# A long convolution's Toeplitz pipeline: an order left to a scheduler, and one written out in slots of four channels

## The chip, the core and the metric

The kernel runs on one core of one Trainium2 chip. TensorE multiplies matrices, VectorE (DVE in the profile) and ScalarE (ACT) work elementwise, GpSimd (POOL) and SyncE (SP) here mostly issue transfers. The metric is the device time of one launch in microseconds.

## The reference

The program is a model of two layers, each with two mixers and a feed-forward part, over x of 2 sequences, 2048 tokens and 256 channels, in f32. The change lies in one mixer of the second layer, and only that matters here:

- x is normalized and projected to 512 inner channels and 512 gates: `xz = norm(x) @ W_in.T`.
- The inner channels go through a causal convolution of four taps with a bias, then Silu: xs.
- Each channel is convolved, causally along its sequence, with a kernel of its own, 1024 taps long (`k_ssm`): y.
- `(y + D_skip * xs) * silu(gate)` is projected back by `W_out` and added to x.

## The kernel before

The method is `sublayer_c`. The 4096 tokens are cut into eight chunks of 512 (`NCH`, `CH`), the 512 inner channels into four blocks of 128 (`E`, index e).

The long convolution is a matmul for each channel. With the sequence in tiles of 128 tokens, tile i of y is the sum over nine shifts m of a 128 x 128 Toeplitz matrix and tile i - m of x. The channel's x, 16 tiles of two sequences, is the stationary operand of 32 columns; a piece of 128 columns of the channel's Toeplitz rows streams past it. Four channels share the array, each with 32 output partitions, so a group of four channels is 4 x 9 matmuls (`convolve`, L1160). Each f32 matmul has two records in the trace. A block has 32 groups, the stage 128. Four groups fill a PSUM tile and leave together (`leave`, L1171: one copy by ScalarE and one transfer to DRAM, c_yd); four groups are called a quartet below.

The Toeplitz rows of a group are made by `kernels` (L1102) in a tile toep of 128 partitions x 4 channels. Two transfers bring 32 partitions each, one for two of the channels on SyncE's queue, one for the other two on ScalarE's. In each half the other 96 partitions are shifted copies: two by VectorE (L1111, L1112), two by ScalarE (L1113, L1114), the second of each pair reading what the first wrote. The pool c_kb has three such tiles, so the loads for a group can start only when the convolution three groups before is done.

Beside that, one chunk's work for the block after (`produce`, `turn`) and the block before (`finish`, `project`) is put into each quartet. `produce` (L1128) projects a chunk (TensorE, L1133), copies it to SBUF (ScalarE, c_xi, L1139), runs the four taps (VectorE, c_acc, L1142 and L1144) and Silu (ScalarE, c_xs, L1146), and writes c_xs to DRAM; `turn` (L1150) transposes it and VectorE puts it into the ring c_x (L1156). `finish` (L1178) reads y and xs back through GpSimd's queue, makes the gate (TensorE, L1186; ScalarE's Silu, L1188), and joins them on VectorE (L1189, L1190); `project` (L1193) multiplies by W_out into ps_o and adds to x (L1201). c_xi, c_acc, c_xs, c_yc and ps have two or three buffers, ps_o one.

Block 0 has no finished block beside it, block 3 none to produce; block 0 is produced ahead of the loop, block 3 is finished behind it.

In what order an engine works is settled by `manual_schedule`. Before, it names TensorE only: TensorE follows the order of the program's text, and a scheduler arranges the others by its own estimates, also across the bounds of stages. Each engine's own stream is then fixed: an instruction that waits holds up all behind it.

Of the kernel before, what the change touches and what calls it, by code (L numbers as in the profile page):

```python
# [17 lines left out]
AF = mybir.ActivationFunctionType  # L18
ALU = mybir.AluOpType
AX = mybir.AxisListType  # L20
PSUM = bass.MemoryType.PSUM
DRAM = bass.MemoryType.DRAM

P = 128
# [4 lines left out]
CH = 512  # L29
NCH = NT // CH  # L30
# [29 lines left out]
def new(pool, shape, name, **kw):  # L60
    return pool.tile(list(shape), F32, name=name, tag=name, **kw)


class Kernel:
# [1007 lines left out]
    def sublayer_c(self):  # L1072
# [7 lines left out]
        tc, nc = self.tc, self.nc  # L1080
        V, A, G = nc.vector, nc.scalar, nc.gpsimd
        E, TAPS = 4, L_CONV // P
        Q = P // 4
        W = L_CONV + P + P - Q
        with ExitStack() as c:
            dp = c.enter_context(tc.tile_pool(name="c_dram", bufs=1, space=DRAM))
            yd = dp.tile([E * P, NB, B, P], F32, name="c_yd", tag="c_yd")
            xd = dp.tile([E * P, NT], F32, name="c_xd", tag="c_xd")
            kp = c.enter_context(tc.tile_pool(name="c_k", bufs=1))
            xT = new(kp, [P, 2, NT], "c_xT")  # L1090
            wi = self.load(kp, "C_W_inT", pat="(k p) n -> p k n", p=P)
            wo = self.load(kp, "C_W_outT", pat="(k p) n -> p k n", p=P)
            cw = self.load(kp, "C_conv_w", pat="(k p) n -> p k n", p=P)
            cb = self.load_cols(kp, "C_conv_b")
            dk = self.load_cols(kp, "C_D_skip")
            xring = [new(kp, [P, P, TAPS + NB, B], f"c_x{j}") for j in range(2)]
            for t in xring:
                G.memset(t[:, :, 0:TAPS], 0.0)
            kb = c.enter_context(tc.tile_pool(name="c_kb", bufs=3))
            kr = self.a["C_krev"]  # L1100

            def kernels(e, g):  # L1102
                t = new(kb, [P, 4, W], "toep")
                for r in range(2):
                    first = kr.offset + (e * P + 4 * g + 2 * r) * KREV
                    (nc.scalar if r else nc.sync).dma_start(
                        out=t[r * (P - Q) : r * (P - Q) + Q, 2 * r : 2 * r + 2],
                        in_=bass.AP(kr.tensor, first, [[1, Q], [KREV, 2], [1, W]]),
                    )
                a, b = t[:, 0:2], t[:, 2:4]  # L1110
                V.tensor_copy(a[Q : 2 * Q, :, 0 : W - Q], a[0:Q, :, Q:W])  # L1111
                V.tensor_copy(a[2 * Q : P, :, 0 : W - 3 * Q], a[0 : 2 * Q, :, 2 * Q : W - Q])  # L1112
                A.copy(b[2 * Q : 3 * Q, :, Q:W], b[3 * Q : P, :, 0 : W - Q])  # L1113
                A.copy(b[0 : 2 * Q, :, 3 * Q : W], b[2 * Q : P, :, Q : W - 2 * Q])  # L1114
                return t

            with tc.tile_pool(name="c_ln", bufs=2) as lp, tc.tile_pool(name="c_pl", bufs=2, space=PSUM) as pl:
                self.norm_transpose(lp, pl, lambda i: self.x[:, i, :], list(range(NI)), xT)
            tp = c.enter_context(tc.tile_pool(name="c_t", bufs=2))
            xp = c.enter_context(tc.tile_pool(name="c_xin", bufs=3))  # L1120
            pp = c.enter_context(tc.tile_pool(name="c_ps", bufs=2, space=PSUM))
            pt = c.enter_context(tc.tile_pool(name="c_pt", bufs=1, space=PSUM))
            pc = c.enter_context(tc.tile_pool(name="c_pc", bufs=2, space=PSUM))
            po = c.enter_context(tc.tile_pool(name="c_po", bufs=1, space=PSUM))
            c.enter_context(tc.manual_schedule(engines={mybir.EngineType.PE}))
            last = [None]

            def produce(e, ch):  # L1128

                b, i0, cs = ch // 4, ch % 4 * 4, slice(ch * CH, (ch + 1) * CH)  # L1130
                ps = new(pp, [P, CH], "ps")
                for k in range(2):
                    nc.tensor.matmul(ps, wi[:, k, e * P : (e + 1) * P], xT[:, k, cs], start=k == 0, stop=k == 1)  # L1133
                xin = new(xp, [P, 3 + CH], "c_xi")
                if i0 == 0:
                    V.memset(xin[:, 0:3], 0.0)
                else:
                    V.tensor_copy(xin[:, 0:3], last[0][:, CH : CH + 3])
                A.copy(xin[:, 3:], ps)  # L1139
                last[0] = xin  # L1140
                acc = new(tp, [P, CH], "c_acc")
                V.tensor_scalar(acc, xin[:, 0:CH], cw[:, e, 0:1], cb[:, e : e + 1], ALU.mult, ALU.add)  # L1142
                for j in range(1, 4):
                    V.scalar_tensor_tensor(acc, xin[:, j : j + CH], cw[:, e, j : j + 1], acc, ALU.mult, ALU.add)  # L1144
                xs = new(tp, [P, CH], "c_xs")
                A.activation(xs, acc, AF.Silu)  # L1146
                G.dma_start(out=xd[e * P : (e + 1) * P, cs], in_=xs)
                return e, ch, xs

            def turn(e, ch, xs):  # L1150

                b, i0 = ch // 4, ch % 4 * 4
                ps = new(pt, [P, 4, P], "ps_t")
                for j in range(4):
                    nc.tensor.transpose(ps[:, j, :], xs[:, j * P : (j + 1) * P], self.ident)
                V.tensor_copy(  # L1156
                    xring[e % 2][:, :, TAPS + i0 : TAPS + i0 + 4, b], ps.rearrange("p j c -> p c j")
                )

            def convolve(e, g, t, ps):  # L1160
                x = xring[e % 2]
                for m in range(TAPS + 1):
                    for j in range(4):
                        lo = L_CONV - m * P + j // 2 * (P - Q)
                        nc.tensor.matmul(  # L1165
                            ps[j * 32 : (j + 1) * 32, g % 4, :],
                            x[:, 4 * g + j, TAPS - m : TAPS - m + NB, :].rearrange("p i b -> p (i b)"),
                            t[:, j, lo : lo + P], start=m == 0, stop=m == TAPS,
                        )

            def leave(e, g, ps):  # L1171

                ys = new(tp, [P, 4, P], "c_ys")
                A.copy(ys, ps[:, :, ::-1])
                rows = slice(e * P + 4 * g, e * P + 4 * g + 16)
                A.dma_start(out=yd[rows].rearrange("(s j) i b t -> (j i b) s t", j=4), in_=ys)

            def finish(e, ch):  # L1178
                b, i0, cs = ch // 4, ch % 4 * 4, slice(ch * CH, (ch + 1) * CH)
                yc, xs = new(tp, [P, CH], "c_yc"), new(tp, [P, CH], "c_xs")  # L1180
                G.dma_start(out=yc.rearrange("p (i t) -> p i t", t=P), in_=yd[e * P : (e + 1) * P, i0 : i0 + 4, b])
                G.dma_start(out=xs, in_=xd[e * P : (e + 1) * P, cs])
                ps = new(pp, [P, CH], "ps")
                z0 = E * P + e * P
                for k in range(2):
                    nc.tensor.matmul(ps, wi[:, k, z0 : z0 + P], xT[:, k, cs], start=k == 0, stop=k == 1)  # L1186
                sz = new(tp, [P, CH], "c_acc")
                A.activation(sz, ps, AF.Silu)  # L1188
                V.scalar_tensor_tensor(yc, xs, dk[:, e : e + 1], yc, ALU.mult, ALU.add)  # L1189
                V.tensor_tensor(yc, yc, sz, ALU.mult)  # L1190
                return e, ch, yc

            def project(e, ch, yc):  # L1193
                for j0 in range(0, 4, 2):
                    ps = new(po, [P, 2, D], "ps_o")
                    for j in (j0, j0 + 1):
                        nc.tensor.matmul(
                            ps[:, j - j0], yc[:, j * P : (j + 1) * P], wo[:, e, :], start=True, stop=True
                        )
                    i = ch * 4 + j0  # L1200
                    V.tensor_tensor(self.x[:, i : i + 2, :], self.x[:, i : i + 2, :], ps, ALU.add)  # L1201

            due = []

            def later(step, *todo):

                for f, args in due:
                    f(*args)
                due[:] = [(step, a) for a in todo]

            for ch in range(NCH):
                t = produce(0, ch)
                later(turn, t)
            later(turn)
            for e in range(E):
                for g in range(P // 4):
                    t = kernels(e, g)
                    if g % 4 == 0:
                        ps = new(pc, [P, 4, P], "ps_c")
                    convolve(e, g, t, ps)  # L1220
                    if g % 4 == 3:
                        leave(e, g - 3, ps)
                    if g % 4 == 0:
                        work = []
                        if e + 1 < E:
                            work.append((turn, produce(e + 1, g // 4)))
                        if e > 0:
                            work.append((project, finish(e - 1, g // 4)))
                    elif g % 4 == 2:
                        for f, args in work:  # L1230
                            f(*args)
            for ch in range(NCH):
                t = finish(E - 1, ch)
                later(project, t)
            later(project)


    def ternary_weights(self, pool):
# [459 lines left out]
```

## Time and profile before

| | us |
|---|---|
| median of 3 runs | 13912.62 (13908.2 to 13919.0) |
| profiled execution | 13913.98, its span 13912.3 |
| norm ahead of the stage | 10969.9 to 11012.5 |
| eight chunks of block 0 | 11012.5 to 11051.8 |
| 128 groups | 11051.8 to 11938.3 |
| end of block 3 | 11938.3 to 11986.0 |

In the profile, PE is TensorE's matmuls and PEld its weight loads; a q behind an engine's name is its queue of transfers, whose issue does not count as busy. A line of instructions gives start, length, engine, line, operation, output and inputs, and in brackets the idle time ahead of it and what ended that. A line of waits gives the engine and what waited, what it waited for, the sum in us, how often, and the longest. PEclk is the granted clock of TensorE as a part of the full one.

### The profile page before, as it was taken

To read this page: it belongs to the slowest core of one execution; us is meant where nothing else is said; L and a number is where in the kernel's file an instruction comes from. 1 tells how busy PE (TensorE), PEld (TensorE's weight loads), DVE (VectorE), ACT (ScalarE), POOL (GpSimd) and SP (SyncE) were. 2 spreads that over 40 slices of the span, in tenths; PEclk is the share of its full clock that TensorE was granted. 3 is DMA by queue.
4 is the path that set the end of the run, shared out by engine and by line. 5 is a ranking of instruction groups with operands and counts; after the bars stand their busy time and mean duration, and the time that the engine had idled before them with its cause. 6 is when DMAs were issued, how large, how long until landed. Compare 5 with 4: busy or idle time off the path is not lost. (4 is left out here: it accounts for less than half of the span.)

```text
span 13912.3 us, 263001 instructions
## 1 busy us (share of the span) xinstructions
PE 5521.0 (40%) x66344; PEld 3798.1 (27%) x66344; DVE 10663.1 (77%) x65491; ACT 9306.1 (67%) x45234; POOL 432.4 (3%) x496
## 2 busy tenths in 40 slices
PE   4222222222222222222222222222289766778888
PEld 2111111111111111111111111111255444544445
DVE  6888888888888888888888888888857655555555
ACT  3777777777777777777777777777626366434444
POOL 0000000000000000000000000000000000131110
PEclk7555555555555555555555555555579778889999
DMA  3000000000000000000000000000000144242210
GB/s 80 14 15 16 17 14 17 14 17 17 14 17 14 17 17 14 17 14 17 17 14 17 14 17 17 14 17 14 14 13 1 41 123 132 62 94 35 33 32 19
DMA packets 334776, 382.28 MB, mean 27 GB/s; under 512 B 207074, under 2 KB 247081, under 8 KB 332212
## 3 DMA queue, kind: packets, MB, share of 16 engines
q1 hardware_dynamic: 289204, 281.11, 8.8%
q10 hardware_dynamic: 29184, 49.82, 1.3%
q0 software_dynamic: 14848, 34.36, 0.9%
q8 instruction: 533, 8.73, 0.3%
q14 instruction: 1007, 8.25, 0.2%
HBM read 307.96 MB, written 52.46 MB: 26 GB/s over the span
## 5 line engine op out<-in xcount | busy, mean ns | idle before, releaser
L410 PE MATMUL hc<-hs,mean 128*32 128x2 f32 x16384 | 588.2, 203 | 7116.8 <-DVE hs L480 7052.2
L410 PEld LDWEIGHTS hc<-hs,mean 128*32 128x32 f32 x16384 | 412.7, 140 | 7328.8 <-DVE hs L480 7263.8
L475 DVE TENSOR_TENSOR p<-p,ir 128x64 f32<-128x64 f32 x4096 | 739.0, 222 | 1065.4 <-ACT ir L463 1065.4
L459 ACT ACTIVATE lm<-m 128x64 f32<-128x64 f32 x2048 | 466.2, 228 | 1216.3 <-DVE m L451 1216.3
L493 PE MATMUL yps<-cs,hist 128*64 128x8 f32 x8192 | 1225.0, 259 | 13.0 <-DVE hs L480 13.0
L391 ACT ACTIVATE bx<-dx,tc 128x64 f32<-128x64 f32 x4098 | 1169.4, 332 | 0.1
L1522 ACT ACTIVATE d_p<-ps_e 128x512 f32<-128x512 f32 (+3 forms) x1280 | 599.4, 537 | 756.1 <-PE ps_o L1503 534.2
L493 PEld LDWEIGHTS yps<-cs,hist 128*64 128x64 f32 x8192 | 1033.2, 218 | 45.1 <-DVE hs L480 13.4
L418 ACT ACTIVATE sq<-hc 128x2 f32<-128x2 f32 x2048 | 353.2, 172 | 794.0 <-PE hc L410 794.0
L480 DVE CUSTOM_DVE_ANT_0 hist<-p,sg 128x64 f32<-128x64 f32 x4096 | 764.5, 224 | 22.5 <-ACT rm L470 4.2
L442 DVE TENSOR_TENSOR p<-p,fac 128x64 f32<-128x64 f32 x4096 | 741.6, 222 | 8.9 <-DVE p L437 6.6
L477 DVE SCALAR_TENSOR_TENSOR p<-e,p 128x64 f32<-128x64 f32 x4096 | 740.6, 222 | 9.9 <-ACT sg L469 7.8
L444 DVE TENSOR_TENSOR p<-p,bx 128x64 f32<-128x64 f32 x4096 | 727.5, 219 | 2.5
L439 ACT ACTIVATE fac<-ngd,ci 128x64 f32<-128x64 f32 x2048 | 711.8, 348 | 1.0 <-DVE p L436 1.0
L436 DVE SCALAR_TENSOR_TENSOR p<-hist,ea 128x64 f32<-128x64 f32 x2048 | 461.1, 225 | 321.8 <-ACT ea L429 321.8
L429 ACT ACTIVATE ea<-ex 128x64 f32<-128x64 f32 x2048 | 524.3, 256 | 102.7 <-DVE ex L424 7.0
L1515 PE MATMUL ps_e<-d_qt,d_kt 128*128 128x512 f32 (+3 forms) x1280 | 558.1, 445 | 44.3 <-ACT d_p L1522 35.5
L472 ACT ACTIVATE ld<-e 128x64 f32<-128x64 f32 x2048 | 548.2, 268 | 0.0
L410 PE MATMUL hd<-hs,mean 128*32 128x2 f32 x16384 | 544.3, 193 | 0.0
L473 ACT ACTIVATE k<-rm 128x64 f32<-128x64 f32 x2048 | 544.1, 266 | 0.0
L1472 PE MATMUL ps_m<-d_kt,d_qt 128*128 128x512 f32 (+3 forms) x1280 | 499.9, 438 | 99.1 <-DVE d_part L1477 39.9
L1165 PE MATMUL ps_c<-toep,c_x 128*32 128x128 f32 x9216 | 407.5, 341 | 306.6 <-ACT toep L1114 304.9
(452 smaller groups left out, 22795.9 us busy)
## 6 DMA issues: line engine op xcount, KB each, us to landing
ng<-dtd SPq DMA_DIRECT2D x258, 256.0 KB, 3.7
dx<-dxd SPq DMA_DIRECT2D x258, 256.0 KB, 4.2
toep<-in_C_krev ACTq DMA_DIRECT2D x128, 312.0 KB, 4.7
toep<-in_C_krev SPq DMA_DIRECT2D x128, 312.0 KB, 4.7
d_kt<-d_kd SPq DMA_DIRECT2D x128, 128.0 KB, 4.1
d_qt<-d_qd SPq DMA_DIRECT2D x128, 128.0 KB, 3.8
y<-ys SPq DMA_DIRECT2D x512, 8.0 KB, 1.9
c_xd<-c_xs POOLq DMA_DIRECT2D x32, 256.0 KB, 4.5
```

The lines of the kernel that those rows point to most:

```text
L391: A.activation(bx[o][:, k2], tg[j][2][:, k], AF.Identity, scale=tg[j][0][:, k2, k : k + 1], bias=0.0 if k2 else SMALL,)
L410: nc.tensor.matmul(out[r : r + 32], mean[:, r : r + 32], hs[i], start=True, stop=True)
L439: A.activation(fac, ngd, AF.Exp, scale=ci)
L442: V.tensor_tensor(p[:, k2], p[:, k2], fac, ALU.mult)
L444: V.tensor_tensor(p[:, k2], p[:, k2], bx[o][:, k2], ALU.add)
L472: A.activation(ld, e, AF.Ln, scale=-1.0, bias=1.0)
L475: V.tensor_tensor(p[:, k2], p[:, k2], ir, ALU.mult)
L477: V.scalar_tensor_tensor(p[:, k2], e, -1.0, p[:, k2], ALU.add, ALU.mult)
L480: V.tensor_tensor_reduce(out=hn[:, k2], in0=p[:, k2], in1=sg, scale=-1.0, scalar=0.0 if k2 else J * SMALL, op0=ALU.mult, op1=ALU.add, accu ...
L493: nc.tensor.matmul(yps[:, k, :], hist[g][:, k, k2], tg[g][3][:, k2, k], start=k2 == 0, stop=k2 == 1)
L1515: nc.tensor.matmul(s[:, q0:], ks[kt // 4][:, hh, kt % 4 * P : (kt % 4 + 1) * P], q[:, hh, q0:], start=True, stop=not diag,)
L1522: A.activation(pr[:, q0:], s[:, q0:], AF.Exp, scale=0.25)
```

## The change

`manual_schedule()` now holds for all engines. The closures are cut into smaller steps, and the loop over 128 slots writes out in what order every engine meets them. In slot s:

- SyncE issues both loads for slot s+2 (`load_toep`); ScalarE issues none.
- TensorE first gets a piece of the chunk work: in slot 0 of a quartet the projection of the next block's chunk (`x_project`), in slot 1 the gate of the block before (`y_gate`), in slot 3 the transposes (`x_turn`) and the output projection (`y_project`); then it convolves slot s.
- VectorE and ScalarE fill the Toeplitz tile for slot s+1 (`fill_toep`), then take their share of the chunk: in slot 0 the copy out of the quartet before (`leave`), the loads of y (`y_load`), the copy c_xi and two taps (`x_first`); in slot 1 the gate's Silu (`y_silu`) and two taps (`x_rest`); in slot 2 the Silu of c_xs (`x_silu`) and the join (`y_join`); in slot 3 the ring (`x_keep`) and the add (`y_add`).

The write of c_yd goes through GpSimd's queue instead of ScalarE's. ps_o has two buffers instead of one. The first Toeplitz tile is filled behind the eight chunks of block 0. c_kb keeps its three tiles.

```diff
-                    (nc.scalar if r else nc.sync).dma_start(
+                    nc.sync.dma_start(
...
+            def fill_toep(s):
+                t = toeps[s]
                 a, b = t[:, 0:2], t[:, 2:4]
                 V.tensor_copy(a[Q : 2 * Q, :, 0 : W - Q], a[0:Q, :, Q:W])
+                A.copy(b[2 * Q : 3 * Q, :, Q:W], b[3 * Q : P, :, 0 : W - Q])
                 V.tensor_copy(a[2 * Q : P, :, 0 : W - 3 * Q], a[0 : 2 * Q, :, 2 * Q : W - Q])
-                A.copy(b[2 * Q : 3 * Q, :, Q:W], b[3 * Q : P, :, 0 : W - Q])
                 A.copy(b[0 : 2 * Q, :, 3 * Q : W], b[2 * Q : P, :, Q : W - 2 * Q])
...
-            po = c.enter_context(tc.tile_pool(name="c_po", bufs=1, space=PSUM))
-            c.enter_context(tc.manual_schedule(engines={mybir.EngineType.PE}))
+            po = c.enter_context(tc.tile_pool(name="c_po", bufs=2, space=PSUM))
+            c.enter_context(tc.manual_schedule())
...
-                A.dma_start(out=yd[rows].rearrange("(s j) i b t -> (j i b) s t", j=4), in_=ys)
+                G.dma_start(
+                    out=yd[4 * s : 4 * s + 16].rearrange("(s j) i b t -> (j i b) s t", j=4), in_=ys
+                )
...
+            load_toep(0)
+            load_toep(1)
+            x_project(0, 0)
             for ch in range(NCH):
...
+                x_first(0, ch)
+                if ch + 1 < NCH:
+                    x_project(0, ch + 1)
+                if ch:
+                    x_turn()
+                    x_keep(0, ch - 1)
+                x_rest(0)
+                x_silu(0, ch)
+            fill_toep(0)
+            x_turn()
+            x_keep(0, NCH - 1)
+            out = None
+            for s in range(32 * E):
+                e, q, r = s // 32, s % 32 // 4, s % 4
+                more, done = e + 1 < E, e > 0
+                if s + 2 < 32 * E:
+                    load_toep(s + 2)
+                if r == 0:
+                    before, out = out, new(pc, [P, 4, P], "ps_c")
+                    if more:
+                        x_project(e + 1, q)
+                elif r == 1 and done:
+                    y_gate(e - 1, q)
+                elif r == 3:
+                    if more:
+                        x_turn()
+                    if done:
+                        y_project(e - 1)
+                if s + 1 < 32 * E:
+                    fill_toep(s + 1)
+                convolve(s, out)
+                if r == 0:
+                    if before is not None:
+                        leave(s - 4, before)
+                    if done:
+                        y_load(e - 1, q)
+                    if more:
+                        x_first(e + 1, q)
+                elif r == 1:
+                    if done:
+                        y_silu()
+                    if more:
+                        x_rest(e + 1)
+                elif r == 2:
+                    if more:
+                        x_silu(e + 1, q)
+                    if done:
+                        y_join(e - 1)
+                else:
+                    if more:
+                        x_keep(e + 1, q)
+                    if done:
+                        y_add(q)
+            leave(32 * E - 4, out)
+            y_load(E - 1, 0)
+            y_gate(E - 1, 0)
             for ch in range(NCH):
...
+                y_silu()
+                y_join(E - 1)
+                if ch + 1 < NCH:
+                    y_gate(E - 1, ch + 1)
+                y_project(E - 1)
+                if ch + 1 < NCH:
+                    y_load(E - 1, ch + 1)
+                y_add(ch)
```

## The prediction

> **What bounds the kernel now.** I first found where the edited code runs: the time of the long convolution, cut into norm, first chunks, 128 groups and end (busy time by stretch).
>
> ```profile
> core 0: us, PE busy (x) PEld busy (x) DVE busy (x) ACT busy (x) POOL busy (x), PEclk, DMA share, GB/s
> 10969.90:11012.50 42.60, 17.45 (x64) 10.89 (x64) 36.55 (x127) 22.88 (x26) 3.44 (x2) 0.50 0.33 83
> 11012.50:11051.80 39.30, 24.97 (x66) 11.69 (x66) 26.52 (x48) 10.90 (x17) 4.51 (x8) 0.80 0.13 53
> 11051.80:11938.30 886.50, 558.79 (x9696) 424.43 (x9696) 497.80 (x489) 595.83 (x353) 62.78 (x74) 0.78 0.45 123
> 11938.30:11986.00 47.70, 33.99 (x104) 18.42 (x96) 21.77 (x33) 5.36 (x9) 9.24 (x14) 0.93 0.26 83
> ```
>
> The third row is 886.5 us for 128 groups, 6.93 us each. Nobody is full: ScalarE is busy 595.8 (67%), TensorE 559 at a granted clock of 0.78, VectorE 498, the transfers 45%. So it is a loop of waits. Then the waits of that stretch, TensorE's first, then ScalarE's.
>
> ```profile
> PE ps_c L1165 <- ACT toep L1114: 304.9, 79, 6.9
> ...
> ACT c_xi L1139 <- PE ps L1133: 75.1, 20, 7.7
> ACT c_xs L1146 <- DVE c_acc L1144: 59.6, 23, 4.3
> ACT toep L1113 <- DMA toep<-in_C_krev: 53.8, 38, 5.0
> ACT c_ys L1174 <- PE ps_c L1165: 40.2, 32, 5.8
> ACT c_acc L1188 <- PE ps L1186: 28.7, 8, 4.2
> ```
>
> TensorE waits 305 us for ScalarE's copies; ScalarE idles 291 us, most of it (75 + 60 + 40 + 29) for somebody who waits for it. The reason is its order, seen in the timeline of one quartet (four groups) of it:
>
> ```profile
> 11410.37 0.36 ACTq L1106 DMA_DIRECT2D toep<-in_C_krev  x1
> 11410.92 0.39 ACTq L1176 DMA_DIRECT2D c_yd<-c_ys  x1
> 11414.22 0.59 ACT L1139 COPY c_xi<-ps 128x512 f32<-128x512 f32 x1 [3.33 <-PE ps L1133]
> 11414.83 2.21 ACT L1113 COPY toep<-toep 32x2432 f32<-32x2432 f32 x1
> 11417.07 0.60 ACT L1188 ACTIVATE c_acc<-ps 128x512 f32<-128x512 f32 x1
> 11417.69 2.11 ACT L1114 COPY toep<-toep 64x2304 f32<-64x2304 f32 x1
> 11419.83 2.21 ACT L1113 COPY toep<-toep 32x2432 f32<-32x2432 f32 x1
> 11425.25 0.63 ACT L1146 ACTIVATE c_xs<-c_acc 128x512 f32<-128x512 f32 x1 [3.21 <-DVE c_acc L1144]
> ```
>
> The copy c_xi stands ahead of the next Toeplitz copy and waits for a matmul; the second copy of a pair (L1114) stands behind the Silu of c_xs, which waits for four VectorE taps. Meanwhile TensorE has nothing. Each quartet pays this; the next c_ys transfer comes at 11439.2, so a quartet is 28.3 us.
>
> **The change, part by part.** Sums are made on the profiled run: 13914.0 us for a span of 13912.3; it lies 1.4 above the median of the runs shown, 13912.6.
>
> *Same work, new order.* No matmul, copy or activation is added or dropped. I count ScalarE: a Toeplitz pair is 2.21 + 2.11 + two handovers of 0.02 = 4.36 us. A quartet adds c_ys 0.59, c_xi 0.59, Silu c_xs 0.63, and Silu of the gate 0.60 where a previous block is finished. Block 0 (no gate): 17.44 + 1.85 = 19.3. Blocks 1 and 2: 19.9. Block 3 (no x work): 18.65. With 8, 16 and 8 quartets: 154 + 318 + 149 = 622 us. That is the floor. VectorE is under it: pair 1.42 + 1.35 + 0.03 = 2.80, and per quartet 0.16 + 0.55 + 3 x 0.75 + 0.69 + 0.75 + 0.69 + 2 x 0.69 = 6.5, so 4.4 per slot against 4.98. TensorE: convolution 2.17 at full clock, and per quartet 1.88 (x) + 1.88 (gate) + 0.66 (turn) + 2.06 (output) = 6.5; 15.2 per quartet, 19 if a quarter slower.
>
> In the new order a slot's ScalarE work is: pair for the next slot, then one small piece whose input was made a slot earlier or at the head of this one. The 75, 60, 40 and 29 us should go. What is late next is the Toeplitz load.
>
> *The loads.* There are still three buffers, so the load for slot s+3 leaves when convolution s has ended; "two ahead" moves no release. What it has is: SyncE 0.1 + two issues of 0.31 (now both on SyncE; ScalarE gets rid of 128 issues and of the waits that stood ahead of its copies), then landing. The trace has medians of 4.5 (SyncE) and 4.7 (ScalarE), and up to 7.7 beside other transfers. A block 1 quartet moves 4 x 624 + 4 x 256 KB; in 22 us that is 160 GB/s against 138 now, so I take 5.0: 5.7 from release to landed.
>
> Step one quartet of blocks 1 and 2, time 0 where ScalarE begins slot 3 (its Silu of c_xs has just ended). TensorE turns and projects, 2.72 x 1.25 = 3.4, convolves 2.7 to 6.1. The buffer's next load lands at 11.8. ScalarE wants it after slot 3 (4.36) and slot 0 (5.54), at 9.9: about 2 us of stall. The load behind slot 0 (ends 11.2, lands 16.9) then meets a ScalarE that is there at 16.8; the others are in time. So about 22.0 per quartet. Block 0 and 3 lack one heavy TensorE piece; the same steps leave 0.2 and 0.45. Sum: 622 + 16 x 2.1 + 8 x 0.65 = 661, and 4 for the three block changes, where the first readback of y waits for the last write: **665 us, 221 less.**
>
> *TensorE's clock, the factor 1.25.* The trace: convolutions take 2.17 at full clock and up to 4.06 cold; after an idle of 2.5 us one came at 2.17 (at 11083), others at 3.70 and 4.06 after 2.55 and 2.80. The Trainium skill (TensorE: Matmul & The Clock Gate, Part 1) says that the clock falls to half after an idle window of some 3.4 us and is full after as long a busy one. New gaps are under 2.7, so by the rule factor 1: the same steps give 635. By the rows, between 1 and 1.5 (716). I take 1.25; both ends stay in the range.
>
> *Output write moved from ScalarE's to GpSimd's queue.* ScalarE loses 32 issues of 0.39; GpSimd gets them, ahead of the two y loads of the same slot. The trace: c_xs loads take 538 ns to issue at the end of the stage, but a median of 1447 in the middle, where one starts beside VectorE's Toeplitz copies. The skill (SBUF — State Buffer, "SBUF: two separate sides") speaks against this move: a DMA of GpSimd's queue can't write its descriptors while VectorE runs such an f32 copy, 620 ns growing to 3100. By the row each of three issues may take 0.9 more: y landed about 13 us after slot 0 began, when VectorE gets to the join (10.5 + 2.8). That costs nothing, barely. By the page's figure (estimate, +2.5 each) it is some 4 to 5 us late in each of 24 quartets, about 100 us. I take the row.
>
> *Ahead of the loop.* Three Toeplitz pairs now sit inside the norm (six ScalarE copies, 12.9 us, six VectorE, 8.4), some of it on its chain (the reciprocal at 10988.4 is 2.2 late, the group at 11003.4 waits 3): without them 6 us less. In return the first pair (4.36) comes after the last Silu, and the chunk chain is tap, Silu 0.63, copy 0.59, then 3.4 of VectorE: about 4.8 x 8 + 7 against 39.3. +6. Together 0; between -8 and +8.
>
> *The end.* 47.7 us now, with a period of 5.1 us per chunk since y loads come one behind another; two output buffers (po) and loads a chunk ahead leave join 1.44 + project 1.3 + add 1.38 = 4.1, plus a slower first write: -5.
>
> Sum: 13914.0 - 221 - 5 + 0 = 13688, on the median 13687.
>
> **The rivals.**
> *ScalarE alone is the limit.* If the clock stays full and loads land in 4.5, little but the floor stays: about 626, so 13648. For: the rule on the clock. Against: the 7.7 us landings.
> *Late y.* The join in slot 2 waits for loads held up in GpSimd's queue; TensorE's project stands ahead of its convolution. 665 + 100: 13790. For: 1447 against 538. Against: only one issue in three was slowed.
> *Cold TensorE.* Factor 1.85 everywhere: 7.0 per slot in blocks 1 and 2, 824 in all, 13847. Against: TensorE would then be busy nearly without a gap, and the trace shows full clock after such stretches.
> *Slower: the load loop.* Both loads on one queue, with the release tied to the third convolution before: at factor 1.25 the stage passes today's 886 by over 0.2% of the kernel once landing takes 12 us, since every microsecond more adds some 40 to the 128 slots. That would be 919 and over, 13941 or more. For: the engines wait for toep transfers now (120 us VectorE, 54 ScalarE). Against: no landing over 7.7 in the stretch that I looked at, transfers at half load.
> That the loads aren't earlier at all is true already, and in the sum.
>
> **How the numbers follow.** The forecast 0.60, ScalarE alone 0.14, late y 0.13, cold 0.07, slower 0.06. A measurement tells about 0.2%, 28 us, from no change. Faster: all but the last, 0.93; 0.02 for ends that just cancel; slower 0.05. The range runs from ScalarE alone, 13645, to past late y, 13800.
>
> **What would show it.** Right: the convolution stretch 640 to 700 us; ScalarE busy near 90% in it with the same 596 to 615 us; waits of ScalarE for c_acc and ps gone, what is left named toep load, once per quartet in blocks 1 and 2; TensorE clock above 0.85. Wrong: VectorE waiting for c_yc or c_xs in every quartet (late y); convolutions of 4 us (cold); toep landings over 7 us. An end over 13,885 would say that the order of ScalarE was not the cause.

## The result, and the profile after

The changed kernel takes 13715.1 us (median of 4 runs, 13709.0 to 13722.1) against 13911.9 before: a ratio of 0.9857, with a 95% interval of 0.9845 to 0.9870. That is 197 us less; 226 were forecast, and the range held it. The profiled run is 13713.6 us, its span 13711.9.

The same four stretches after (busy time by stretch; norm, first chunks, 128 groups, end):

```profile
core 0: us, PE busy (x) PEld busy (x) DVE busy (x) ACT busy (x) POOL busy (x), PEclk, DMA share, GB/s
10961.30:10994.20 32.90, 17.42 (x64) 10.58 (x64) 28.19 (x121) 9.94 (x20) 3.45 (x2) 0.50 0.43 107
10994.20:11039.80 45.60, 28.20 (x68) 12.44 (x68) 31.61 (x51) 14.62 (x20) 4.65 (x8) 0.76 0.11 47
11039.80:11738.70 698.90, 503.94 (x9694) 381.80 (x9694) 509.98 (x493) 603.46 (x357) 89.31 (x103) 0.86 0.59 155
11738.70:11783.70 45.00, 32.76 (x96) 19.32 (x96) 21.90 (x33) 5.36 (x9) 11.04 (x17) 0.90 0.30 100
```

The third row has nearly all of it: 886.5 us became 698.9. ScalarE has the same work (603 us) in less time, 86% busy instead of 67%. The norm takes 9.7 us less, the first chunks 6.3 more, the end 2.7 less: together -6. So the stage accounts for 194 us of the two profiled runs' 200; the rest lies ahead of the stage and behind it.

ScalarE's waits in the groups, after:

```profile
ACT toep L1118 <- DMA toep<-in_C_krev: 39.7, 20, 3.6
ACT toep L1118 <- DVE c_acc L1144: 18.4, 9, 2.4
ACT toep L1118 <- issue: 16.1, 6, 4.1
ACT c_ys L1194 <- PE ps_c L1185: 6.7, 3, 2.5
ACT toep L1118 <- DVE toep L1117: 3.4, 2, 2.9
```

The waits for taps and projections are nearly gone. What is left stands ahead of L1118, the first copy of a pair, which needs only its load and its buffer; the names behind the arrow change, the waiting instruction doesn't. It is some 80 us of load: in blocks 1 and 2, where ScalarE stalls, L1118 begins 0.1 us after the load that it needs has landed (median). TensorE's longest waits, after:

```profile
PE ps_t L1171 <- ACT c_xs L1164: 96.3, 24, 7.0
PE ps_c L1185 <- ACT toep L1120: 43.8, 32, 2.7
```

The 305 us for ScalarE's Toeplitz copies have become 44. The first row was 3.2 us before: now the transposes at the head of slot 3 wait for the Silu of c_xs, which stands on ScalarE behind a Toeplitz pair, and the convolution of slot 3 waits behind the transposes.

Measured from one c_ys copy to the next, a quartet takes 19.4 us in block 0, 23.7 and 24.0 in blocks 1 and 2, 19.7 in block 3; 19.5, 22.0 and 19.1 were forecast.

A stretch of block 1 (timeline, all engines) shows where the blocks in the middle lose it:

```profile
11294.08 0.76 POOL L1195 DMA_DIRECT2D c_yd<-c_ys  x1 [8.35 <-ACT c_ys L1194]
11294.84 0.76 POOL L1203 DMA_DIRECT2D c_yc<-c_yd  x1
11295.59 0.55 POOL L1204 DMA_DIRECT2D c_xs<-c_xd  x1
...
11302.98 1.42 DVE L1117 COPY toep<-toep 32x2432 f32<-32x2432 f32 x1 [2.64 <-DMA toep<-in_C_krev]
...
11305.06 2.21 ACT L1118 COPY toep<-toep 32x2432 f32<-32x2432 f32 x1 [3.65 <-DMA toep<-in_C_krev]
```

In slot 0 three transfers of GpSimd's queue start within 1.5 us; right then a convolution ends and lets the two Toeplitz loads go. They left at 11295.7 and 11296.1. VectorE, which needs the first, begins 7.3 us after that left, when it has landed; the second landed 8.9 us after it left, and ScalarE, which needs it, begins 9.0 after that, having stood for 3.65. Over blocks 1 and 2 the view of the tile gives (min, median, max)

```profile
DMA to landing us min/median/max: 3.6/6.0/8.9
```

but it knows the landing of only 48 of the 128 loads there, all of them of two of a quartet's four slots. Counted from the completion records of all 128 loads in the trace, the landing is 3.3 at the least, 5.0 in the median and 8.9 at most, where the forecast took 5.0 throughout. It depends on the slot. The second load of a pair, the one that ScalarE needs, has these medians: behind the convolution of slot 0 7.5 us, of slot 1 6.0, of slot 2 4.9, of slot 3 4.4.

ScalarE stalls before two of the four tiles of a quartet in blocks 1 and 2: 2.0 us on the mean before the tile loaded behind slot 3's convolution, which itself comes late, and 1.7 before the tile loaded behind slot 0's, whose load is slow. Before the other two it stands 0.1 or less. The forecast's steps had the first (about 2 us) and gave the second nothing (0.1).

### The profile page after: what moved, and what is told of

Read it like the earlier page. It is cut to its first block, busy times and chain, and to the rows that moved or that the text cites. A ratio compares the mean times of both kernels' runs of the same rounds, so it can differ in the third digit from the quotient of the medians.

```text
span 13711.9 us, 263042 instructions
## 1 busy us (share of the span) xinstructions
PE 5477.8 (40%) x66344; PEld 3762.0 (27%) x66344; DVE 10653.5 (78%) x65491; ACT 9294.0 (68%) x45234; POOL 460.9 (3%) x528
## 5 line engine op out<-in xcount | busy, mean ns | idle before, releaser
L432 PE MATMUL hd<-ident,ci 128*1 128x1 f32 x4096 | 386.7, 163 | 357.2 <-DVE ex L424 303.4
```

## Experiments

Two theories stood after the result. *The load loop*: with three buffers a load leaves when the convolution three slots before has ended, and the way from there to the next copy is just too long. *Late y*: the join of slot 2 waits for c_xs (32 us in 10 joins), and the output projection, TensorE's next convolution and the release of a buffer wait behind it. Of the two waits of TensorE that bear on it, the one for the join is small (17.4 us ahead of ps_o); the one for the Silu of c_xs (96.3 us) belongs to the loop. Times of the 128 groups run from the first convolution to the end of the last and are from one trace each; the whole kernel's are medians, except for the fourth buffer and the five runs that take the change apart, which ran once. Landings are counted from the completion records of all loads of a stretch.

**TensorE convolves first.**

```diff
-                if r == 0: x_project ... elif r == 1: y_gate ... elif r == 3: x_turn, y_project
                 if s + 1 < 32 * E:
                     fill_toep(s + 1)
                 convolve(s, out)
+                if r == 0: x_project ... elif r == 1: y_gate ... elif r == 3: x_turn, y_project
```

> TensorE convolves first in every slot and takes the chunk pieces (projection, gate, transposes, output projection) behind it; nothing else moves. Theory 1, the load loop: in blocks 1 and 2 the buffer of a slot comes free late because up to 3.4 us of chunk pieces stand ahead of the convolution; ScalarE's 81 us of waits ahead of the first Toeplitz copy fall below 40, quartets of blocks 1 and 2 go from 23.7 us to 20.5 to 21.5, the 128 groups from 699 to about 655. Theory 2, late y: the join still waits for its c_xs load and VectorE's next Toeplitz copy behind it, so the groups gain 10 us at most.

Measured: the groups 637.8 us, quartets of blocks 1 and 2 19.9; the kernel 13660.8 us (ratio to before 0.9811, interval 0.9795 to 0.9827). ScalarE's waits:

```profile
ACT c_xi L1152 <- PE ps L1137: 7.5, 12, 1.8
ACT c_acc L1216 <- PE ps L1210: 6.7, 4, 3.9
ACT toep L1118 <- DMA toep<-in_C_krev: 5.6, 6, 2.9
```

VectorE's join still waits, 37.5 us for c_xs instead of 32.3, and it costs next to nothing. Both stalls of ScalarE are gone (0.02 us each on the mean). So the loop is right, late y as a cause by itself is not: once the convolution doesn't stand behind the small pieces, the late join is not on the path. The edit does one thing more: the y transfers, which left within the last 1.5 us of slot 0's convolution, now leave 2.2 to 3.7 us after its end (medians), behind the Toeplitz loads. The load that ScalarE needs lands in 4.5 us there instead of 7.5; that behind slot 1 is slow in its place (6.5), but has room: ScalarE comes for it 1.5 us after it has landed.

**Loads of y a slot earlier.**

```diff
-                    if done:
+                    if done and q == 0:
                         y_load(e - 1, q)
...
                         y_add(q)
+                        if q + 1 < NCH:
+                            y_load(e - 1, q + 1)
```

> The loads of y and xs for a chunk are issued one slot earlier (end of slot 3 of the quartet before, except for the first chunk of a block). Theory 2, late y: VectorE's 32 us of waits for c_xs and most of TensorE's 34 us for VectorE's copies go, quartets of blocks 1 and 2 fall by 1.5 us or more, the groups by 25 to 35 us. Theory 1, the load loop: the join was not on the path; 10 us at most.

Measured: the groups 654.3, the kernel 13683.0 (0.9824, 0.9808 to 0.9841): 45 us from the groups, more than late y alone was to give. The wait for c_xs fell to 9.2 us. But the Toeplitz loads gained too: the y loads now leave some 8 to 9 us before the convolution of slot 0 ends, and the second load behind it lands in a median of 4.9 us in blocks 1 and 2 instead of 7.5. The stall before that tile is gone (0.04 us on the mean instead of 1.7), the one behind slot 3 stays (1.8). This run doesn't tell late y from the slow loads; the one before and the fourth buffer below do.

**The write of c_yd back on ScalarE's queue.**

```diff
-                G.dma_start(out=yd[4 * s : 4 * s + 16]...
+                A.dma_start(out=yd[4 * s : 4 * s + 16]...
```

> The write of c_yd is back on ScalarE's queue, everything else as changed. If GpSimd's queue is what makes y late (c_xs now lands in a median of 7.1 us, 5.5 before), c_xs lands about 1 to 1.5 us sooner, VectorE's waits for it halve, and the groups gain 10 to 25 us. If the queue is not the cause, the landing stays near 7 and ScalarE pays 32 issues of 0.39: same or up to 12 us more.

Measured: the groups 666.4, the kernel 13692.9 (0.9834, 0.9817 to 0.9850). c_xs lands in 3.8 us instead of 7.1, the Toeplitz loads of blocks 1 and 2 in 4.4 instead of 5.0. On GpSimd's queue the write had stood in front of the y loads and waited for c_ys; without it they leave some 9 us before slot 0's convolution ends, not beside its end. As with y early, the stall behind slot 0 goes (0.05 us) and the one behind slot 3 stays (1.5). ScalarE does pay for its issues, since none can leave before the copy c_ys has ended:

```profile
ACT c_xi L1152 <- ACT c_ys L1194: 8.4, 19, 0.5
```

This part of the change was a loss of some 32 us all the same, by one trace of each; by whole runs the intervals of the two ratios overlap a little.

**A fourth buffer.** The room for it comes from leaving out half the norm.

```diff
-            xT = new(kp, [P, 2, NT], "c_xT")
+            xT = new(kp, [P, 2, NT // 2], "c_xT")
-            kb = c.enter_context(tc.tile_pool(name="c_kb", bufs=3))
+            kb = c.enter_context(tc.tile_pool(name="c_kb", bufs=4))
...
-   xT[:, k, ch * CH : (ch + 1) * CH]
+   xT[:, k, ch % 4 * CH : (ch % 4 + 1) * CH]
```

> A fourth Toeplitz buffer. To make room for it the norm and its transposes are done for the first sequence only and both sequences are projected from it (so half the norm, some 16 us, is left out), and c_xi has two buffers. Only the 128 groups are to be read. Theory 1, the load loop: a load then leaves a slot earlier, ScalarE's 81 us of waits for toep nearly vanish, quartets of blocks 1 and 2 are near ScalarE's floor, 20 to 21 us, the groups 635 to 650. Theory 2, late y: 10 to 20 us of gain at most, the join's waits stay.

Measured: the groups 633.0, blocks 1 and 2 19.8 and 20.0 per quartet. ScalarE waits 2.1 us in all for loads, while the join waits for c_xs longer than ever:

```profile
ACT toep L1118 <- DMA toep<-in_C_krev: 2.1, 5, 0.5
DVE c_yc L1220 <- DMA c_xs<-c_xd: 48.0, 14, 8.7
```

The loads are no quicker than as changed (5.4 us in the median of blocks 1 and 2, 5.0 as changed), they only leave earlier. This is the cleanest proof of the loop: in the groups the text, the queues and the order are as changed, a load leaves a slot earlier, and c_xi has one buffer less, which can only hold work up. (The whole kernel's 13639.5 us is short of half a norm and is not compared.)

**Both: convolve first, y early.**

> TensorE convolves first in every slot, and y's loads are issued a slot earlier: both edits together. If late y and the late release of the buffer are one chain (y late, so the output projection late, so the convolution behind it late, so the load late), breaking it twice gives little over breaking it once: the groups 625 to 638 us against 638 with the first edit alone. If they are two separate losses they add up: about 593, which is under ScalarE's floor of 622 and so is not expected.

Measured: the groups 630.5, the kernel 13661.8 (0.9814, 0.9798 to 0.9831), no difference to convolving first alone that these runs can tell. Not additive: one chain, and under it ScalarE's work, 606.5 us busy of 630.5.

**Is ScalarE then the floor?** Beside both edits, VectorE makes the copies c_xi and c_ys.

```diff
-                A.copy(ys, ps[:, :, ::-1])
+                V.tensor_copy(ys, ps[:, :, ::-1])
-                A.copy(xin[:, 3:], held["x"])
+                V.tensor_copy(xin[:, 3:], held["x"])
```

> As the kernel with both edits, and the copies c_xi and c_ys are made by VectorE instead of ScalarE (24 x 0.59 and 32 x 0.58 us). If ScalarE's work is the floor of the groups now (606 us busy of 638), its 33 us come off nearly whole: the groups 600 to 610 us, ScalarE near 573 busy, VectorE near 547. If the load loop or VectorE bounds, nothing is gained: 630 or more.

Measured: the groups 615.4, a gain of 15 of the 33 us forecast (the 618 of the next text counts on to the c_ys copy behind the last convolution); ScalarE 579 us busy (573 forecast), VectorE 541. Block 0 went from 139 to 129 us (seven quartets), blocks 1 and 2 stayed (160 and 157 for eight), block 3 rose from 144 to 150. ScalarE was the floor of block 0; in the middle another limit was right below it, VectorE or, with 18.0 us of ScalarE's waits, the loads.

> TensorE convolves first, y's loads go a slot earlier, c_xi is copied by VectorE, c_ys by VectorE in block 0 only and by ScalarE elsewhere. With both copies on VectorE blocks 1 and 2 stayed at 157 to 160 us per eight quartets, where VectorE had 2.8 x 4 + 7.8 = 19.0 us of work in a quartet. If VectorE bounds them there, handing c_ys back to ScalarE brings 155, block 3 goes from 150 to 144, block 0 stays at 129: the groups about 610 us, against 618. If something else holds blocks 1 and 2 (loads, y), they stay at 158 and the groups near 615.

```diff
+                (V.tensor_copy if s < 32 else A.copy)(ys, ps[:, :, ::-1])
```

Measured: the groups 612.5 (610 forecast), blocks 1 and 2 155.7 and 156.6, block 3 147.7 (144 forecast). That is 3 us under the kernel with both copies on VectorE, too little in one trace each to say that VectorE was the limit there. The kernel takes 13635.9 us (5 runs, 13629.4 to 13641.4), 0.9800 of before (0.9786 to 0.9813), the fastest of all; its interval overlaps with those of the versions with TensorE convolving first, with both edits and with both copies on VectorE.

```profile
11045.90:11658.40 612.50, 480.53 (x9689) 358.81 (x9689) 526.85 (x524) 589.58 (x326) 106.52 (x103) 0.94 0.66 177
```

ScalarE is busy 96% of the groups here. With this much work on ScalarE, no order can give more than the other 23 us.

**What made the gain?** Five runs took the change apart.

The text of before with the order of all engines fixed, `manual_schedule()` and nothing else:

> The kernel before, with the order of its text fixed for all engines (the one word changed in the schedule). In that text the load on ScalarE's queue stands right ahead of the copy that needs it, and a chunk's Silu right behind the taps it waits for. If the order is what counts and the fixing alone does nothing good: each slot pays landing 4.7 and pair 4.4 on ScalarE in turn, each quartet some 8 more for the chunk: 40 us and more per quartet, the groups 1200 to 1500 us, some 400 us slower than before. If fixing the order is the gain in itself: the groups 700 us.

Measured: the groups 1448.7, the kernel 14498.7 us. ScalarE's timeline in it:

```profile
11414.14 0.32 ACTq L1106 DMA_DIRECT2D toep<-in_C_krev  x1
11417.44 2.21 ACT L1113 COPY toep<-toep 32x2432 f32<-32x2432 f32 x1 [1.20 <-DMA toep<-in_C_krev]
11419.68 2.11 ACT L1114 COPY toep<-toep 64x2304 f32<-64x2304 f32 x1
11419.69 0.32 ACTq L1106 DMA_DIRECT2D toep<-in_C_krev  x1
...
11436.37 0.58 ACT L1174 COPY c_ys<-ps_c 128x512 f32<-128x512 f32 x1 [8.78 <-PE ps_c L1165]
```

Each load leaves right ahead of the copy that needs it, and c_ys holds up everything until its convolution is done. Fixing an order gains nothing in itself; the scheduler had done better with that text.

The new text, but ScalarE, VectorE and the queues arranged by the scheduler again:

> The changed kernel, but only TensorE's order is fixed; the scheduler arranges ScalarE, VectorE and the queues again. If it is ScalarE's and VectorE's written order that gains: the groups go back by 60 us or more, to 760 to 890. If TensorE's new order and the moved queues gain it: 690 to 720 as with the change.

Measured: the groups 743.1, the kernel 13776.0. That lies between the two forecasts: 143.4 of the 187.6 us come without any written order of ScalarE and VectorE, the written order adds 44.2. ScalarE waits again, but less than before: 71.1 us for ps_c at c_ys, 41.8 for taps.

The text of before with the moved queues alone (both loads on SyncE, c_yd on GpSimd, two output buffers):

> The kernel before with the moved queues alone: both Toeplitz loads on SyncE, the write of c_yd on GpSimd, two output buffers; TensorE's order and the scheduler as before. The new text left to the scheduler took 743 us for the groups, so 143 of the 187 us came without any written order of ScalarE and VectorE. If the queues made them (ScalarE no longer stops at an issue whose buffer isn't free): 745 to 790. If TensorE's new order and the smaller pieces made them: 850 to 886.

Measured: the groups 826.9, the kernel 13846.1. The moved queues and the second output buffer give 60 us; neither forecast.

The new text with TensorE's order alone fixed and the queues of before:

> The changed text with the queues of before (every second load and the write of c_yd on ScalarE's) and only TensorE's order fixed: the smaller pieces and TensorE's order alone. If these made the 143 us: 740 to 780. If the queues did: 840 to 886. The two shares of this run and of the queues alone should add up to about 143 unless they are one chain.

Measured: the groups 670.2, the kernel 13695.2: better than the forecast, and 29 us better than the whole change. The new text with the queues of before gives 216 us. What it has beside the old text is more than smaller pieces: the loads stand two slots and the fills one slot ahead, c_ys is copied a slot later, and ps_o has its second buffer here too. TensorE's order differs little: in blocks 1 and 2 of the traces before and as changed it is the same except for the projection of the next chunk, which has moved from behind slot 0's convolution to ahead of it. Which of these makes the 216 us was not told apart. ScalarE's waits with the scheduler in charge:

```profile
ACT toep L1120 <- issue: 28.4, 16, 2.8
ACT toep L1118 <- issue: 15.0, 6, 2.9
...
ACT toep L1118 <- DMA toep<-in_C_krev: 8.4, 3, 6.1
ACT c_xi L1152 <- PE ps L1137: 4.6, 1, 4.6
```

The waits for taps and projections are nearly gone here as well. The shares don't add up: the queues that gain 60 us in the old text lose 73 in the new one. (In these two pairs the scheduler arranges anew for each text, so they compare arrangements too.)

The written order with every second load back on ScalarE's queue:

```diff
-                    nc.sync.dma_start(
+                    (nc.scalar if r else nc.sync).dma_start(
```

> The changed kernel with every second load back on ScalarE's queue, all orders written out. ScalarE then stands at the head of each slot until the convolution two slots back is done, and pays an issue of 0.33. By the steps of the forecast the convolution ends up to 1.8 us after ScalarE gets there, once or twice a quartet: 128 x 0.33 + 24 x 2, the groups 740 to 790. If the queue is of no account in a written order: 695 to 705.

Measured: the groups 664.3, the kernel 13687.5, 35 us less in the groups where 40 to 90 more were expected. Of ScalarE's 128 issues 98 cost nothing, since they go out while ScalarE still copies:

```profile
11317.08 2.11 ACT L1120 COPY toep<-toep 64x2304 f32<-64x2304 f32 x1
...
11318.44 0.37 ACTq L1109 DMA_DIRECT2D toep<-in_C_krev  x1
11319.10 0.58 ACT L1194 COPY c_ys<-ps_c 128x512 f32<-128x512 f32 x1
```

and the wait that was feared is there (35.2 us for convolutions), but the wait for landings is nearly gone (1.5 us). c_xs lands in 5.1 us instead of 7.1. The loads land in 4.1 us (SyncE's) and 4.5 (ScalarE's) over all blocks instead of 4.6, a small gain; the large one is in the load behind slot 0 that ScalarE needs, 4.4 instead of 7.5 in blocks 1 and 2. But the y transfers leave 1.6 to 3.1 us after the end of slot 0's convolution here (medians), behind the Toeplitz loads, and as changed within the last 1.5 us before its end, ahead of them. The Trainium skill (DMA: Bandwidth & Descriptors, "Issuing engines are not separate DMA queues") says that another issuing engine saves only the time to issue. This run doesn't contradict it: whether the second queue itself has a part, or only the other moments at which the transfers leave, was not told apart.

## Why the prediction was right, and by what it missed

- *The cause: ScalarE's order.* Right. In the versions made from the new text its waits for taps, projections and convolutions (204 us in four rows before) shrink to 11 as changed and 134 at most. But that the order is written out was only a quarter of it, 44 of 188 us: from the new text the scheduler finds as good a one (670 us with the old queues), and what in that text does it stays open.
- *ScalarE's floor, 622 us.* Right: 630.5, 633.0 and 637.8 once the loop is opened, and less only when work is taken off ScalarE (612.5).
- *The load loop: right mechanism, one load mis-sized.* "So I take 5.0" held as a median over blocks 1 and 2. The term that failed is "the load behind slot 0 (ends 11.2, lands 16.9)": 5.7 us from release to landed, for which ScalarE was to come in time. There the load that ScalarE needs took 8.0 us in the median and 7.4 on the mean, since it leaves together with the three y transfers, and the stall of 0.1 became 1.7. That is most of the 1.9 us by which a quartet of blocks 1 and 2 is longer than forecast; 16 of them are 30 of the 34 us by which the groups passed 665, block 3 most of the rest. The other stall, behind slot 3, was forecast at about 2 us and measured 2.0, but by luck: the convolution of slot 3 ended 7.0 us in the median after the Silu of c_xs, not 6.1, and its load landed 4.9 after that, not 5.7.
- *TensorE's clock, factor 1.25.* Right in blocks 0 and 3, where a convolution was busy 2.69 us on the mean against 2.17 at full clock (1.24); too careful for the convolutions of blocks 1 and 2, for which the steps were made: 2.29 us, 1.06. There the transposes and the projection of slot 3 made up for it: the convolution behind them began 4.5 us after the Silu (median), not 3.4. The granted clock was 0.86. The premise "new gaps are under 2.7" failed: 16 gaps of TensorE were over 3.4 us, the longest 7.0, most of them the waits for the Silu of c_xs. So the run does not try the rule of the Trainium skill (TensorE: Matmul & The Clock Gate, Part 1: the clock falls after an idle window of some 3.4 us). The kernel with c_ys on VectorE in block 0 only does: none of its gaps is over 3.0 us, and 19 of its 128 convolutions were still busy for over 3.5 us.
- *Output write on GpSimd's queue: named as free, barely, but a loss of some 32 us.* The row was the right one for the price of an issue: c_yc and c_xs take 1.03 and 0.87 us to issue on the mean, not 2.5 more, as the estimate from the Trainium skill (SBUF — State Buffer, "SBUF: two separate sides") had it. The page's mechanism is in the trace all the same: it has such an issue blocked until VectorE's instruction ends, and 27 of the 28 slowed ones end 0.12 or 0.31 us after a Toeplitz copy of VectorE does. But such a copy is only 1.35 to 1.42 us long. The loss came by another way than either: the write waits for c_ys at the head of GpSimd's queue and moves both y loads to where the Toeplitz loads leave.
- *Late y, 13790*: the join did wait (32.3 us), but as a cause by itself it is refuted: with a fourth buffer it waits 48.0 us, and the groups take 633.0.
- *Loads on SyncE: "ScalarE gets rid of 128 issues and of the waits"* had the wrong sign as it stands: with half of the loads back on ScalarE's queue the groups are 35 us shorter.
- *Norm and first chunks 0, end -5*: -3.4 and -2.7.
- *Slower, cold TensorE*: neither came near. "Toep landings over 7 us", named as a sign of being wrong, did come, 13 of 250 in the groups (8 before), the longest 8.9 us, not 12.

## What to carry to other kernels

Before an order is written out, step through one period with each engine's own durations, and ask of every buffer when it is released and what stands ahead of that on the releasing engine: here a text in which loads and copies stand ahead of their slot gave most of the gain even with the scheduler in charge of ScalarE and VectorE, and putting TensorE's small pieces behind the long job instead of ahead of it gained another 61 us. A landing time taken from a calm stretch doesn't hold for the slot in which several transfers start at once; look at the slot, not at the median, and ask of how many transfers a median knows. And taking issues off a busy engine need not be a gain: an issue that lies beside a running instruction cost nothing here, one that must wait for that instruction's result cost 0.44 us.

## What was not expected of the hardware

Two loads of 312 KB left one behind the other on one queue, right after three transfers of 256 KB. The second landed 8.9 us after its issue, the first at most 7.3, against 3.3 at the least for a load of blocks 1 and 2, at a mean of 155 GB/s over the stage. In four other arrangements the second load behind slot 0 lands in 4.4 to 4.9 us in the median instead of 7.5: in two the y loads leave 8 to 9 us before the convolution of slot 0 ends, in two all three y transfers leave 1.6 to 3.7 us after its end. And a write that waits for its data at the head of GpSimd's queue delays the reads behind it: with it c_xs left beside the Toeplitz loads and landed in 7.1 us, without it 9 us earlier, and landed in 3.8.
